# Result layout over the DMA parts, a gate half copied out by ScalarE, and a moved filter group in a GNN layer kernel

## The chip, the cores and the metric

The kernel runs on one core of a Trainium2 chip. The core has TensorE (PE in the profile; PEld is its weight load), VectorE (DVE), ScalarE (ACT), GpSimd (POOL) and SyncE (SP)[...]. Transfers are issued from SP and POOL here and run on 16 DMA engines. The metric is device time in microseconds for one execution of the whole program, less is better; the median of three runs before the change is 1708.58 us (1705.66 to 1714.0).

## The reference

`x` is 64 graphs of 256 nodes with 256 features, `adj` 64 matrices of 256 x 256. One layer is computed, all in float32:

```python
h = jnp.maximum(_layernorm(x, axis=-1), 0.0)
# convolution branch over the node axis
c = relu(bn(conv1d(h^T, conv1_w, 0)))
c = bn(conv1d(c, conv2_w, 8))                  # 17 taps
x_conv = relu(c + h^T)^T
# message branch
s = h @ w_se.T + b_se
A = exp(-dist(s, s)) * adj
x_nmp = A @ relu(h @ w_msg.T + b_msg)
# GRU cell, input is the two branches, state is h
gi = concat([x_conv, x_nmp]) @ w_ih.T + b_ih
gh = h @ w_hh.T + b_hh
r = sigmoid(gi_r + gh_r); z = sigmoid(gi_z + gh_z)
n = tanh(gi_n + r * gh_n)
return x + (1 - z) * n + z * h
```

## The kernel before

The 64 graphs are worked in 32 pairs, and four pairs make a batch (8 batches). Features lie on partitions in most of the work, so `HT[i]` holds pair i's `h` transposed, two chunks (`dc`) of 128 features by 512 columns.

The 17-tap convolution is done in a transformed domain. The taps are turned into filters once, at the start (`filters`, called by `filter_steps`), and written to DRAM (`filt`); each batch then reads them again, 47 loads of 256 KB into nine slots `wb` (`load_kinds`, `product`). In a batch `begin(m)` opens a product in a PSUM pair of banks `acc` (two of these, used in turn), ACT copies its first half to the second, and `complete(m)` adds two more products and lets ACT move the result out. The message branch (`message`, `embed`, `affinity`, `aggregate`) is spread between; it uses four single PSUM banks `aux` in turn and leaves `x_nmp` in `XNM[i]`, a ring of two tiles.

The gates of a pair are `gates(i)`: `seven` computes a 2 x 2 block product with seven block products, into `A` and `E` (the two `acc`), first for the gates r and z, then for the two halves of the gate n. `opened` is called when one of them is whole. For the gate n that is the inner function `n(dc, p)`, from line 1190: ACT takes one half of the PSUM tile with its bias into `gn`; VectorE multiplies it by r; VectorE adds the other half straight from PSUM; ACT applies tanh; three VectorE operations make the new state `d`, in `tr`; and two ACT copies of two-byte elements per `dc` split the words of `d` into their halves, in `back`. `finish(i)` then issues a DMA transpose on SP, `gn<-back`, and `deliver(i)` puts the halves together again (two ACT copies, `back<-gn`), adds `x` to it by two accumulating transfers on POOL, and writes the two graphs to `out` by two more. The last pair of a batch is delivered in the middle of the next batch; the last pair of all goes another way and isn't touched.

A row of `out` or `x` is brought onto partitions in one of two orders: `rows` (partition = 16 h + b) and `blocks` (partition = 8 b + h, which is the order of memory in pieces of two nodes). The access pattern of `rows` has 8 as its outermost dimension, that of `blocks` 16.

No instruction is issued where it is written. The class `Recorder` records every operation with an assumed cost, and `plan` orders them for all engines at once: TensorE in an order near the one written, the others by due times worked back from it, with a simple model of transfers in which `size` (line 346 for accumulating ones) is the time on the DMA engines. All instructions therefore have line 371 in the profile, and are told apart by their tiles.

At the start, pairs 0 to 3 are normalized, transposed and convolved one after the other, and `filter_steps` puts filter groups (line 1298) between them.

Of the kernel before, what the change touches and what calls it, by code (L numbers as in the profile page):

```python
# [14 lines left out]
U16 = mybir.dt.uint16  # L15
AF = mybir.ActivationFunctionType
ALU = mybir.AluOpType
# [232 lines left out]
class Recorder:  # L250
# [83 lines left out]
    def record(self, engine, op, args, kw):  # L334
        method = getattr(getattr(self.nc, engine), op)
        out = kw["out"] if "out" in kw else args[0]
        ins = [v for v in list(args) + list(kw.values()) if isinstance(v, bass.AP) and v is not out]
        n = 1
        for s in out.shape[1:]:
            n *= s  # L340
        size = 0
        if op.startswith("dma"):
            if "transpose" in op:
                size, cost = 2.5, self.TURN
            elif "accum_op" in kw:
                size, cost = 2.3, 1.0
            else:
                k = max(self.share(out, ins[0]), 10 if engine == "gpsimd" else 1)
                run = min(self.run(v) for v in (out, ins[0]))
                size = n * out.shape[0] * WIDTH[out.dtype] * 16 / k / 330e3 * max(1, 1400 / run)  # L350
                cost = 0.35 if k > 10 and run > 1024 else 0.62
        elif engine == "tensor":
            cost = n / 597 + 0.006
            if op == "transpose":
                cost = out.shape[-1] / 1170
            elif args[1].shape[0] < 32:
                cost = 0.23
        elif engine == "vector":
            cost = {"bn_stats": 0.33, "bn_aggr": 0.07}.get(op, n / 960 + 0.07)
            if op == "tensor_mul" and n == 256:  # L360
                cost = 0.5
        elif engine == "scalar":
            cost = n / 1400 + (0.2 if op == "activation" else 0.12)
            if out.dtype == U16:
                cost = n / 860
            elif len(out.shape) == 3 and op == "activation" and n == 256:
                cost = 0.49
        else:
            cost = 1.1 if self.planned == 0 else 7.0 if ALU.pow in args else 2.0
        k = len(self.tasks)  # L370
        self.tasks.append(Task(engine, lambda: method(*args, **kw), cost, size, self.first))  # L371
        self.last[engine] = k
        if self.behind is not None:
            self.tasks[k].preds.add(self.behind)
        if self.first is not None:
            self.first += 1
        for v in ins:
            self.access(k, v, False)
        self.access(k, out, True)
        return k  # L380
# [106 lines left out]
def kernel(  # L487
# [18 lines left out]
    nc = Recorder(tc.nc)  # L506
    P = 128
    B, N, D = x.shape
    G = 2
# [4 lines left out]
    DC = D // P  # L514
# [6 lines left out]
    L = 16  # L521
    NW = N // L
# [65 lines left out]
    def rows(t, g):  # L588
        return t[g].rearrange("(b h c) d -> h b (c d)", h=L // 2, c=MC)

    def row_tile(t, g):
        return t[:, g * MC:(g + 1) * MC, :].rearrange("p c d -> p (c d)")
# [5 lines left out]
    def chunk(t, g, c):  # L598
        return t[:, g * N + c * P:g * N + (c + 1) * P]
# [3 lines left out]
    X, ADJ, HT, XNM, STATS = {}, {}, {}, {}, {}  # L603
# [5 lines left out]
    def blocks(t, g):  # L609
        return t[g].rearrange("(b h c) d -> b h (c d)", h=L // 2, c=MC)  # L610
# [114 lines left out]
    p = aux()  # L725
# [449 lines left out]
    def halfs(p, k):  # L1175
        return p[:, :, k * N:(k + 1) * N]

    def pieces(t):
        return t.rearrange("p (g n) -> p g n", n=N)

    def gates(i, between=None):
        tr, gn = tr_tile, gn_tile
        tz = [slots[ROLE[f"tz{dc}"]].rearrange("p c d -> p (c d)") for dc in range(DC)]

        def rz(dc, p):
            for gate, t in ((0, tr[:, dc]), (1, tz[dc])):
                nc.scalar.activation(pieces(t), halfs(p, gate), AF.Tanh,
                                     bias=b_rz[:, gate * DC + dc:gate * DC + dc + 1], scale=0.5 - dc)

        def n(dc, p):  # L1190
            g = gn[:, dc]
            nc.scalar.activation(pieces(g), halfs(p, 1), AF.Identity,
                                 bias=b_hh[:, 2 * DC + dc:2 * DC + dc + 1], scale=1.0 - 2 * dc)
            nc.vector.scalar_tensor_tensor(g, tr[:, dc], 1.0, g, op0=ALU.add, op1=ALU.mult)
            nc.vector.scalar_tensor_tensor(pieces(g), pieces(g), 0.5, halfs(p, 0), op0=ALU.mult,
                                           op1=ALU.subtract if dc else ALU.add)
            nc.scalar.activation(g, g, AF.Tanh, bias=b_ih[:, 2 * DC + dc:2 * DC + dc + 1])
            d = tr[:, dc]
            nc.vector.tensor_sub(d, HT[i][:, dc], g)
            nc.vector.scalar_tensor_tensor(d, tz[dc], 1.0, d, op0=ALU.add, op1=ALU.mult)  # L1200
            nc.vector.scalar_tensor_tensor(d, d, 0.5, g, op0=ALU.mult, op1=ALU.add)
            u = d.bitcast(U16).rearrange("p (n j) -> p j n", j=2)
            for j in range(2):
                nc.scalar.copy(back.bitcast(U16).rearrange("p (c j n) -> p c j n", c=DC, j=2)[:, dc, j], u[:, j])

        def last(dc, g, p):
            a = slice(g * N, (g + 1) * N)
            v, d = gn[:, dc, a], tr[:, dc, a]
            nc.scalar.activation(v, p[:, N:], AF.Identity,
                                 bias=b_hh[:, 2 * DC + dc:2 * DC + dc + 1], scale=1.0 - 2 * dc)  # L1210
            nc.vector.scalar_tensor_tensor(v, d, 1.0, v, op0=ALU.add, op1=ALU.mult)
            nc.vector.scalar_tensor_tensor(v, v, 0.5, p[:, :N], op0=ALU.mult, op1=ALU.subtract if dc else ALU.add)
            nc.scalar.activation(v, v, AF.Tanh, bias=b_ih[:, 2 * DC + dc:2 * DC + dc + 1])
            nc.vector.tensor_sub(d, HT[i][:, dc, a], v)
            nc.vector.scalar_tensor_tensor(d, tz[dc][:, a], 1.0, d, op0=ALU.add, op1=ALU.mult)
            for c in range(MC):
                t = chunk(y_last[:, dc], g, c).rearrange("p (b h) -> p h b", b=NW)
                u, w = (q[:, c * P:(c + 1) * P].rearrange("p (h b) -> p h b", b=NW) for q in (d, v))
                nc.vector.scalar_tensor_tensor(t, u, 0.5, w, op0=ALU.mult, op1=ALU.add)

        seven(i, RZ, rz)
        if between:
            between()
        if i + 1 < NP:
            seven(i, NH, n)
            return
        a0, p5, e1, a1, e0 = aux(), aux(), aux(), acc()[:, 1], acc()[:, 0]
        e = slots[ROLE["e"]].rearrange("p c d -> p (c d)")
        part(a0, 1, i, NH, True)
        nc.scalar.mul(e0, a0, -1.0)  # L1230
        part(p5, 5, i, NH, True)
        nc.scalar.copy(e, p5)
        part(a0, 2, i, NH)
        last(0, 0, a0)
        part(e0, 6, i, NH)
        nc.vector.tensor_add(a1, e0, e)
        part(e0, 7, i, NH)
        nc.vector.scalar_tensor_tensor(e1, e0, -1.0, e, op0=ALU.mult, op1=ALU.subtract)
        last(1, 1, e1)
        part(a1, 3, i, NH)  # L1240
        last(0, 1, a1)
        part(e0, 4, i, NH)
        last(1, 0, e0)
# [16 lines left out]
    def deliver(i):  # L1260
        y = back.rearrange("p (q d) -> p q d", d=D)
        t = gn_tile.rearrange("p c n -> p (c n)").bitcast(U16)
        v = y.bitcast(U16).rearrange("p q (c d j) -> p j c q d", c=DC, j=2)
        u = t.rearrange("p (c j q d) -> p j c q d", j=2, c=DC, d=P)
        for j in range(2):
            nc.scalar.copy(v[:, j], u[:, j])
        for g in range(G):
            nc.gpsimd.dma_start(out=row_tile(y, g), in_=rows(x, G * i + g), accum_op=ALU.add)
            nc.gpsimd.dma_start(out=rows(out, G * i + g), in_=row_tile(y, g))

    FIRST = PARTS[1][1]
    steps = deque((m, g) for g in range(FIRST) for m in range(len(PASSES)))
# [5 lines left out]
    def filter_steps(n, wide=True):  # L1278
        for _ in range(n):
            banks[0] += 1  # L1280
            p = acc()[:, 0] if wide and banks[0] % 3 == 0 else aux()
            filters(p, *steps.popleft(), nc.gpsimd if len(steps) % 2 else nc.sync)
# [9 lines left out]
    for j in range(PB):  # L1292
        if j > 0:
            norm(j)
        transpose_h(j)
        conv1(j, True)
        split(j)
        filter_steps((1, 2, 3, 3)[j])
    *bn2, b_ih, b_hh = columns("bn2")
    s2, h2_shift = fold_bn(bn2, "bn2", 1.0 / L)  # L1300
    b_rz = keep("b_rz", 2 * DC)
# [19 lines left out]
    for b in range(NB):  # L1321
        i = b * PB
# [25 lines left out]
        if b == 0:  # L1348
# [6 lines left out]
            back = late.tile([P, DC * W], FP, name="back")  # L1355
# [168 lines left out]
```

## Time and profile before

| | |
|---|---|
| runs | 1705.66, 1714.0, 1708.58 us |
| profiled execution | 1703.87 us |
| its span, first to last instruction | 1702.1 us |
| mean granted TensorE clock | 0.994 |
| POOL and SP transfers: `back<-in_x_dram`, `out_dram<-back` | 62 each, 256 KB |
| filter loads `wb<-filt` | 376, 256 KB |

A view of the instructions in order of time gives start, length, engine, tile written and read, and in brackets the idle time of that engine before, with what ended it. Where an instruction waits for several semaphores, the bracket names only one.

### The profile page before, as it was taken

How to read it: one execution, taken by the hardware profiler on the slowest of the kernel's cores; microseconds unless marked ns; L12 is line 12 of the kernel's file. 1: busy time of each engine (PE TensorE's matmuls, PEld its weight loads, DVE VectorE, ACT ScalarE, POOL GpSimd, SP SyncE). 2: the span in 40 equal slices, each digit the busy share in tenths (PEclk: the TensorE clock that was granted, in tenths of full speed). 3: DMA queues.
4: the chain of work that ended last, by engine and by line, in shares of the span. 5: the costliest groups of instructions: out<-in, count | busy, mean ns of one | idle time of the engine just before them, and what ended most of it. 6: DMA issues, size and time to landing. Idle time of an engine off the chain costs nothing.

```text
span 1702.1 us, 26181 instructions
## 1 busy us (share of the span) xinstructions
PE 1666.3 (98%) x8984; PEld 1420.8 (83%) x8984; DVE 1457.8 (86%) x3401; ACT 1052.4 (62%) x1967; POOL 231.8 (14%) x245
## 2 busy tenths in 40 slices
PE   8999999999999999999999999999999999999998
PEld 5888878988889788888888887897888978898886
DVE  7969989799889998799997998979987899879545
ACT  5546665685657765676655866567575766556453
POOL 4211130022110121102110021101211012100010
PEclk9999999999999999999999999999999999999999
DMA  9982666966579366773559554694756836484032
GB/s 228 306 280 69 137 117 142 280 136 140 108 196 241 94 127 124 218 208 89 122 113 293 136 116 110 160 273 97 144 112 191 233 91 125 88 245 129 17 60 52
DMA packets 326812, 261.47 MB, mean 154 GB/s; under 512 B 204751, under 2 KB 252139, under 8 KB 326678
## 3 DMA queue, kind: packets, MB, share of 16 engines
q1 hardware_dynamic: 296982, 216.71, 48.4%
q0 software_dynamic: 29280, 42.76, 13.1%
q8 instruction: 71, 1.16, 0.3%
q14 instruction: 63, 0.52, 0.1%
q10 hardware_dynamic: 416, 0.32, 0.1%
HBM read 156.60 MB, written 43.78 MB: 118 GB/s over the span
## 4 chain that ended last, share of the span: by engine, by line
PE 77%; DVE 17%; DMA 3%; issue 1%; ACT 1%; SPq 0%; DVEq 0%; ACTq 0%
PE acc L371 52%; PE aux L371 25%; DVE V L371 3%; DVE T L371 3%; DVE U L371 2%; DVE gn L371 2%; DMA wb<-filt 2%; DVE tr L371 1%; DVE acc L371 1%; DVE wb L371 1%; DVE Yv L371 1%; DVE PT L371 1%; DMA taps<-in_c_wT_dram 1%; DVE msg L371 1%; DMA filt<-Yv 0%
## 5 line engine op out<-in xcount | busy, mean ns | idle before, releaser
L371 PE MATMUL acc<-wb,w_ih 128*128 128x256 f32 x768 | 191.9, 379 | 0.0
L371 PEld LDWEIGHTS acc<-wb,w_ih 128*128 128x128 f32 x768 | 145.9, 190 | 19.8
L371 POOL DMA_DIRECT2D back<-in_x_dram x62 | 61.9, 1161 | 696.6 <-ACT back L371 622.5
L371 POOL TENSOR_TENSOR rstd<-rstd,neg_half 128x4 f32<-128x4 f32 x32 | 81.6, 2548 | 472.7 <-DVE shift L371 284.8
L371 PE MATMUL aux<-wb,w_x 128*128 128x256 f32 x576 | 141.6, 384 | 0.6 <-ACT e L371 0.5
L371 DVE SCALAR_TENSOR_TENSOR V<-T,V 128x128 f32<-128x128 f32 (+2 forms) x448 | 140.2, 377 | 0.0
L371 PE MATMUL acc<-wb,w_x 128*128 128x256 f32 x576 | 136.5, 381 | 1.8 <-DVE acc L371 1.5
L371 PEld LDWEIGHTS acc<-wb,w_x 128*128 128x128 f32 x576 | 107.9, 190 | 28.6 <-DVE acc L371 8.4
L371 PEld LDWEIGHTS aux<-wb,w_x 128*128 128x128 f32 x576 | 108.0, 191 | 20.2 <-issue 4.0
L371 PE MATMUL aux<-w_msg,hT 128*128 128x259 f32 x512 | 120.9, 381 | 0.0
L371 PE MATMUL acc<-V,wb 128*128 128x128 f32 x1024 | 119.0, 275 | 0.6 <-ACT acc L371 0.6
L371 PEld LDWEIGHTS acc<-U,wb 128*128 128x128 f32 x1024 | 117.4, 192 | 1.5 <-issue 0.5
L371 PE MATMUL acc<-U,wb 128*128 128x128 f32 x1024 | 118.2, 275 | 0.3 <-DMA wb<-filt 0.3
L371 PEld LDWEIGHTS acc<-V,wb 128*128 128x128 f32 x1024 | 116.7, 192 | 1.2 <-ACT acc L371 0.8
L371 PE MATMUL acc<-wb,w_hh 128*128 128x256 f32 x384 | 110.1, 381 | 0.7 <-ACT acc L371 0.7
L371 DVE TENSOR_TENSOR T<-Yv 128x512 f32<-128x512 f32 (+1 forms) x80 | 42.5, 580 | 79.4 <-ACT Yv L371 78.9
L371 PE MATMUL aux<-hT,w_c 128*128 128x512 f32 x224 | 107.3, 595 | 2.7 <-ACT e L371 2.7
L371 PE MATMUL acc<-Yv,w_ih 128*128 128x256 f32 x380 | 108.5, 381 | 0.1
L371 PEld LDWEIGHTS aux<-w_msg,hT 128*128 128x128 f32 x512 | 96.5, 190 | 14.3
L371 PE MATMUL acc<-hT,w_hh 128*128 128x256 f32 x380 | 104.7, 383 | 0.6 <-ACT acc L371 0.4
L371 PE MATMUL acc<-xnm,w_ih 128*128 128x256 f32 x380 | 103.9, 380 | 0.0
L371 ACT COPY back<-gn 128x1024 uint16<-128x1024 uint16 x62 | 80.5, 1348 | 36.6 <-DMA gn<-back 36.6
(194 smaller groups left out, 3842.1 us busy)
## 6 DMA issues: line engine op xcount, KB each, us to landing
wb<-filt SPq DMA_DIRECT2D x376, 256.0 KB
back<-in_x_dram POOLq DMA_DIRECT2D x62, 256.0 KB, 7.3
out_dram<-back POOLq DMA_DIRECT2D x62, 256.0 KB, 4.8
x<-in_x_dram SPq DMA_DIRECT2D x58, 256.0 KB
halves_d<-halves SPq DMA_DIRECT2D x28, 512.0 KB
adjh<-halves_d SPq DMA_DIRECT2D x112, 128.0 KB
hh<-halves SPq DMA_DIRECT2D x108, 128.0 KB
filt<-Yv POOLq DMA_DIRECT2D x18, 224.0 KB, 4.6
```

The costliest lines, as they stand in the source:

```text
L371: self.tasks.append(Task(engine, lambda: method(*args, **kw), cost, size, self.first))
```

## The change

Four edits. The results go to memory and are added to `x` in `blocks` order, for which the last two copies in `n` reorder the columns while they write. In `n`, ACT copies the second half of the gate out of PSUM into `XNM[i][:, dc]` (which is no longer needed there), and VectorE reads that instead of PSUM. The first filter group at the start is asked for after the second pair, not after the first, and one group more after the fourth. The planner's assumed `size` of an accumulating transfer goes from 2.3 to 1.3.

```diff
             elif "accum_op" in kw:
-                size, cost = 2.3, 1.0
+                size, cost = 1.3, 1.0
...
             nc.scalar.activation(pieces(g), halfs(p, 1), AF.Identity,
                                  bias=b_hh[:, 2 * DC + dc:2 * DC + dc + 1], scale=1.0 - 2 * dc)
+            x = XNM[i][:, dc]
+            nc.scalar.copy(pieces(x), halfs(p, 0))
             nc.vector.scalar_tensor_tensor(g, tr[:, dc], 1.0, g, op0=ALU.add, op1=ALU.mult)
-            nc.vector.scalar_tensor_tensor(pieces(g), pieces(g), 0.5, halfs(p, 0), op0=ALU.mult,
-                                           op1=ALU.subtract if dc else ALU.add)
+            nc.vector.scalar_tensor_tensor(g, g, 0.5, x, op0=ALU.mult, op1=ALU.subtract if dc else ALU.add)
...
             u = d.bitcast(U16).rearrange("p (n j) -> p j n", j=2)
+            v = back.bitcast(U16).rearrange("p (c j n) -> p c j n", c=DC, j=2)[:, dc]
             for j in range(2):
-                nc.scalar.copy(back.bitcast(U16).rearrange("p (c j n) -> p c j n", c=DC, j=2)[:, dc, j], u[:, j])
+                nc.scalar.copy(v[:, j].rearrange("p (q b h) -> p q h b", h=L // 2, b=NW),
+                               u[:, j].rearrange("p (q h b) -> p q h b", h=L // 2, b=NW))
...
         for g in range(G):
-            nc.gpsimd.dma_start(out=row_tile(y, g), in_=rows(x, G * i + g), accum_op=ALU.add)
-            nc.gpsimd.dma_start(out=rows(out, G * i + g), in_=row_tile(y, g))
+            nc.gpsimd.dma_start(out=row_tile(y, g), in_=blocks(x, G * i + g), accum_op=ALU.add)
+            nc.gpsimd.dma_start(out=blocks(out, G * i + g), in_=row_tile(y, g))
...
-        filter_steps((1, 2, 3, 3)[j])
+        filter_steps((0, 2, 3, 4)[j])
```

## The prediction

> **What bounds the kernel now.** I read the page first, then who made TensorE (PE) wait, then the instructions in order of time around the longest waits on PE, SP, POOL and ACT.
>
> ```profile
> span 1702.1 us, 26181 instructions
> PE 1666.3 (98%) x8984; PEld 1420.8 (83%) x8984; DVE 1457.8 (86%) x3401; ACT 1052.4 (62%) x1967; POOL 231.8 (14%) x245
> ```
>
> PE is the bound: 1702.1 - 1666.3 = 35.8 us is all that any rearrangement can win. The view of who waited for whom, for PE alone, shows where most of it lies:
>
> ```profile
> PE acc L371 <- DVE tr L371: 9.4, 4, 2.4
> PE acc L371 <- DMA wb<-filt: 3.1, 4, 1.9
> PE aux L371 <- DMA taps<-in_c_wT_dram: 2.7, 1, 2.7
> PE acc L371 <- DVE gn L371: 1.8, 1, 1.8
> ```
>
> The reader should see that four waits of 2.3 to 2.4 us are put down to VectorE. In the instructions in order of time they all stand at one place, the start of a batch (`begin(0)`, first filter product); PE, SP and POOL at the fourth such place:
>
> ```profile
> 896.78 1.04 PE L371 MATMUL aux<-w_msg,hT 128*128 128x259 f32 x4
> 900.22 3.81 PE L371 MATMUL acc<-Sv,wb 128*128 128x128 f32 x32 [2.40 <-DVE tr L371]
> ...
> 893.52 20.01 SPq L371 DMA_DIRECT2D wb<-filt  x23
> ...
> 886.80 1.96 POOL L371 DMA_DIRECT2D back<-in_x_dram  x2 [27.11 <-ACT back L371]
> 893.27 0.64 POOL L371 DMA_DIRECT2D out_dram<-back  x1 [4.51 <-DMA back<-in_x_dram]
> 895.89 0.63 POOL L371 DMA_DIRECT2D out_dram<-back  x1 [1.99 <-DMA back<-in_x_dram]
> ```
>
> The named releaser is misleading. The matmul waits for several semaphores, and the one that is last but for the start itself is the landing of a filter load. Of the sixteen completion marks of the load issued at 893.96, eight come at 896.61 to 897.38 and eight at 898.61 to 900.09; PE starts at 900.22. The result write issued at 893.27 has the same split: eight marks at 896.0 to 896.7, eight at 898.0 to 899.5. So the write sits on half of the DMA engines, and a filter load that needs all sixteen waits for that half. The six places and their waits are 296.45 (1.75), 497.11 (2.28), 697.76 (1.95), 900.22 (2.40), 1101.01 (2.36), 1301.79 (2.36): 13.1 us. The seventh, near 1500, shows under 1 us.
>
> [...] `rows` has an outer dimension of 8, `blocks` of 16 or, merged, 128. The marks above agree with 8. [...] the copy into `zT` stored at a stride of 32 bytes (first four pairs) against the same shape stored densely (later pairs).
>
> ```profile
> L371 ACT COPY zT<-aux x2: 312/355/398, 81.9 to 82.1; 128x128 f32<-128x128 f32 x1, 32x128 f32<-32x128 f32 x1
> ...
> L371 ACT COPY zT<-aux x1: 283/283/283, 304.9 to 304.9; 128x128 f32<-128x128 f32 x1
> ...
> L371 ACT COPY back<-tr x124: 596/618/632, 194.0 to 1671.4; 128x512 uint16<-128x512 uint16 x124
> ```
>
> The first row's 398 ns is the 128x128 form; the four strided ones are 383 to 407 ns, the dense ones of the same places in the batch 254 to 283.
>
> **Part 1, results in block order.** It moves no bytes away; each `back<-in_x` and `out_dram<-back` (62 each, 256 KB) puts 16 KB on sixteen engines instead of 32 KB on eight.
>
> ```profile
> back<-in_x_dram POOLq DMA_DIRECT2D x62, 256.0 KB, 7.3
> out_dram<-back POOLq DMA_DIRECT2D x62, 256.0 KB, 4.8
> ```
>
> At the batch start: the two adds are issued at 886.80 and 887.42 and land at 892.98 and 895.15. Unused engines gave their marks after 2.2 us, so about 4 us of the first add is transfer; halved, it lands near 891 and the second near 893. In the new instruction order ACT runs both `back<-gn` copies ahead of the four `tr`/`tz` evictions (before, two evictions stood between them: 2 x 0.6 us), which brings the adds another 1 us or more forward. The writes then go out near 890 and 892 and half as long per engine, so they are mostly through when the load issued at 893.96 is served; its undelayed half landed by 897.4, before PE is free at 897.82. I take a rest of 0.25 us at each place: 6 x 0.25 = 1.5, a gain of 13.1 - 1.5 = 11.6 us. Bounds: nothing (the half-loaded sixteen collide as badly, a gain of perhaps a third, 4 us) to 13.1. VectorE is not next: the first `acc` is read out by 897.8 and the second half of the gate now is copied out by ACT (part 2).
>
> The price is in the `back<-tr` copies. They now store two-byte elements 16 bytes apart, 124 of them. With a fixed part of 188 ns (the copies of 12 elements into `z` take that), `back<-tr` runs at 0.86 ns an element, `back<-gn` with stores 4 bytes apart at (1348-188)/1024 = 1.13, and the strided `zT` at about 1.74. For 512 elements 1.13 gives 0.77 us, 1.74 gives 1.08. I take 1.02, a growth g of 0.40 us each[...]; bounds 0.15 and 0.46, up to 0.7 if the many short rows cost too (`h<-aux`, rows of 16, takes 782 ns where dense 512-element evictions take about 600). ACT gains 124 x 0.40 = 50 us of work. Most lies in idle time: ACT is at 62%. Two places are tight. Once in each of six batches (440 to 1447), four copies stand right before the exponentials that free the `aux` buffers:
>
> ```profile
> 1039.96 2.17 ACT L371 COPY back<-tr 128x512 uint16<-128x512 uint16 x4
> 1043.28 1.21 ACT L371 ACTIVATE e<-aux 128x256 f32<-128x256 f32 x4 [1.15 <-PE aux L371]
> ...
> 1043.72 1.12 PE L371 MATMUL aux<-hT,w_c 128*128 128x512 f32 x2 [0.45 <-ACT e L371]
> ```
>
> The slack is 1.15 us, of which part 2's copies eat about 0.35; beyond 0.8 each delay of `e` goes to PE directly: 4g - 0.8 = 0.8 us. After a batch start, the four copies stand around the two `Yv<-acc` evictions (before: 904.61 to 906.78), and the second eviction frees the `acc` that `begin(3)` wants at 913.76. Its slack of 1.26 us shrinks because PE runs 2.3 us earlier while the copies still wait for VectorE; I get about 2.2g - 0.2 = 0.7 us. Together 6 x (6.2g - 1.0) = 37g - 6: 8.9 us at g = 0.40, nothing below g = 0.16, 11 at 0.46, 20 at 0.7. The other two groups of four in a batch have 2 to 6 us of idle ACT behind them and cost nothing; without that cover each would cost up to 1.6 us.
>
> **Part 2, gate copied out by ACT.** Adds 62 copies of 128x512 from PSUM; `acc<-acc` of that form takes 575 ns: 35.7 us of ACT. VectorE's product then reads SBUF; `tr<-wb,tr`, all SBUF, takes 679 ns, the PSUM one 677, so nothing. It removes no wait of length: outside the batch starts PE's waits for VectorE at `acc` sum to under 2 us. Behind the copies in ACT's queue stand the evictions of the next pair, which have idle time of 0.5 to 2.7 us ahead of them. Cost beyond the 0.35 us above: 0; bounds -1 to +2 us.
>
> **Part 3, filter group and planner cost.** The first group's wait is for the second `taps` load, landing at 18.69 (PE 18.82, 2.68 us idle). In the new order the transposes come before and the whole group still stands ahead of the second pair's convolution, so PE waits for the same landing with the same work done: 0, bounds -0.5 to +0.5. On SP the `gn<-back` transpose (913.70, 3.32 us) leaves the middle of the filter loads for a place after them; it hid under loads running ahead: 0, bounds -1 to +1. The first batch start has its own new order on SP (an `adj` transpose ahead of the filter loads, in a gap of 12 us before 290.40): 0, bounds -1 to +2.
>
> **Sum.** -11.6 + 8.9 = -2.7 us. Against the profiled execution, 1703.87 (span 1702.1), that is 1701.2. The median of the three runs is 1708.58, 4.7 higher, so there 1705.9.
>
> **Rivals.** Faster: strided stores are cheap (g at or below 0.2). For it: two-byte elements are not four-byte ones, and the `zT` copies are short. Then 37 x 0.2 - 6 = 1.4 and the time is 11.6 - 1.4 = 10.2 lower, 1698. Slower: ACT's queue becomes what PE waits for; one mechanism, the strided copies ahead of `e` and of `Yv<-acc`. At g = 0.75 it costs 21.8, so +10 us, 1719; it outweighs the gain from g = 0.48 and passes +8.5 us from g = 0.71, or from g = 0.5 if the loads still land late (gain 4 only). For it: the rows of 16. Against: 62% ACT. The change does not do what it says: the DMA stays on eight engines or the loads are late for their own length; then only the cost stays, -4 + 8.9 = +5, within the bound. Part 3 is such a case already.
>
> **How the numbers follow.** What one measurement can tell here is about 0.5%, 8.5 us. Forecast (within it) 0.52, with the case of loads still late in it; cheap stores 0.28; ACT bound 0.20. The likeliest case alone: 1700 to 1715. Range 1695 to 1718: it takes in most of the faster case and the lower half of the slower one.
>
> **What would show it.** Right: the waits of about 2.3 us before `acc<-Sv,wb` at six batch starts fall under 0.6; `back<-tr` near 1.0 us; the wait before `aux<-hT,w_c` grows from 0.45 to about 1.2; the `taps` wait stays 2.6. Wrong: `back<-tr` at 0.7 or 1.3; batch starts still at 2 us; new waits of PE for ACT elsewhere.

## The result, and the profile after

The changed kernel takes 1891.94 us (median of 4 runs, 1884.66 to 1896.84) beside 1707.12 us for the kernel before (4 runs, 1702.95 to 1714.0): a ratio of 1.1075, 95% interval 1.1019 to 1.1131. It is 10.8% slower, where 1706 was forecast with a range up to 1718.

The group of the `back<-tr` copies in the kernel before (busy time in us, mean ns of one, idle time before):

```profile
L371 ACT COPY back<-tr 128x512 uint16<-128x512 uint16 x124 | 68.9, 617 | 18.4 <-DVE tr L371 18.4
```

The head of the page of the changed kernel and its busy times, then its costliest group and two rows of the DMA part:

```profile
span 1895.1 us, 26235 instructions
...
PE 1729.3 (91%) x8984; PEld 1465.3 (77%) x8984; DVE 1461.6 (77%) x3401; ACT 1295.1 (68%) x2029; POOL 241.0 (13%) x245
...
L371 ACT COPY back<-tr 128x512 uint16<-128x512 uint16 x124 | 295.4, 2651 | 16.9 <-DVE tr L371 16.7
...
back<-in_x_dram POOLq DMA_DIRECT2D x62, 256.0 KB, 5.3
out_dram<-back POOLq DMA_DIRECT2D x62, 256.0 KB, 2.6
```

PE was 98% busy and is 91% now. One `back<-tr` copy takes 2.65 us where it took 0.62, and the copies fill 295.4 us of ACT where they filled 68.9. (295.4 is less than 124 x 2.651 because one copy begins before the last has quite ended, as at 781.52, where one of 2.46 us is followed by the next at 783.49; a copy holds ACT's queue for 295.4 / 124 = 2.38 us, before for 0.56.) The two transfers land in 5.3 and 2.6 us where they took 7.3 and 4.8, so the sixteen parts do what was meant. ACT is still only 68% busy: its share of busy time does not show that it has become the limit. The view of who made PE wait does (us in total, times, longest):

```profile
PE acc L371 <- ACT wb L371: 39.1, 11, 5.5
PE aux L371 <- ACT e L371: 36.4, 10, 7.0
PE acc L371 <- ACT Yv L371: 35.6, 11, 5.2
PE acc L371 <- ACT acc L371: 22.0, 9, 3.5
PE acc L371 <- DVE acc L371: 14.6, 11, 5.0
...
PE aux L371 <- DMA taps<-in_c_wT_dram: 2.9, 1, 2.9
```

The four rows for ACT hold 133 us; before, the largest row of all was 9.4. The wait for `taps` is still there, as predicted. Of the waits for a filter load at the batch starts, 13.1 us before, none over 0.25 us is left ahead of a batch's first filter product; PE waits for filter loads in two other places, 1.7 us in all (0.44 at 116.27, and 1.28 at 1229.93 ahead of a batch's second filter product). In the transfers' marks at the batch start near 1216, the writes issued at 1215.29 and 1217.27 have landed at 1217.76 and 1219.63, the sixteen marks of each within 0.24 us of one another, and all sixteen marks of the filter loads issued at 1220.55 and 1220.98 come within 0.4 us of one another.

ACT and PE in order of time, at the place that the prediction showed at 1039.96 in the kernel before:

```profile
1149.80 9.28 ACT L371 COPY back<-tr 128x512 uint16<-128x512 uint16 x4
...
1158.59 1.52 ACT L371 ACTIVATE e<-aux 128x256 f32<-128x256 f32 x4
...
1159.35 1.22 PE L371 MATMUL aux<-hT,w_c 128*128 128x512 f32 x1 [6.78 <-ACT e L371]
```

The four copies take 9.28 us instead of 2.17, the exponentials behind them come that much later, and PE, which needs the `aux` bank that they empty, stands for 6.78 us instead of 0.45. From this wait back to the same wait one batch earlier (930.62) lie four other waits, 4.88, 0.94, 5.15 and 2.65 us, and a small one of 0.45. With the 6.78 that is 20.9 us in a batch, beside 2.9 in the kernel before (2.40 and 0.45, from 842.88 to 1043.72). A batch is 228.7 us long instead of 200.8: 27.9 more, and the waits explain 18.0 of it. PE's busy time, 207.9 us in this batch and 198.0 in that one, explains the other 9.9, for the same work.

That rest is TensorE's clock, 0.94 in the mean of this batch and 1.00 in that one. Busy time of each engine in stretches of 7 us that begin where a wait ends, for the changed kernel (columns: stretch; its length; PE, PEld, DVE, ACT and POOL busy with their instructions; granted PE clock; DMA share; GB/s). The waits ahead of the five stretches were 2.65, 6.78, 4.87, 4.96 and 0.45 us:

```profile
1110.70:1117.70 7.00, 7.00 (x26) 5.94 (x27) 3.17 (x6) 6.20 (x4) 4.22 (x2) 0.79 0.19 36
1159.40:1166.40 7.00, 7.00 (x18) 5.08 (x19) 4.14 (x12) 5.63 (x7) 0.00 (x0) 0.61 0.54 116
1210.70:1217.70 7.00, 7.00 (x20) 5.71 (x21) 2.39 (x10) 1.60 (x3) 2.80 (x4) 0.61 0.61 112
...
1245.00:1252.00 7.00, 7.00 (x40) 7.00 (x41) 6.97 (x14) 4.69 (x10) 0.00 (x0) 0.63 0.33 89
1078.80:1085.80 7.00, 7.00 (x32) 6.19 (x33) 7.00 (x19) 4.41 (x7) 2.72 (x1) 1.00 0.11 38
```

After the waits of 4.87, 4.96 and 6.78 us PE is counted as busy, but at 0.61 to 0.63 of its clock over the next 7 us; after 2.65 us at 0.79; after 0.45 at 1.00. From 1118 to 1124 and from 1166 to 1168, behind two of these stretches, it was 1.00 again. By an estimate from these rows, each long wait thus costs 7 x 0.38 = 2.7 us beyond its own length, and a batch loses 7 x (0.39 + 0.39 + 0.37 + 0.21) = 9.5 us so, which is nearly all of the 9.9. How the length of a wait sets the clock behind it is not shown. Over the whole run the mean granted clock fell from 0.994 to 0.951, and PE's busy time grew from 1666.3 to 1729.3 us with the same 8984 matmuls.

### The profile page after: what moved, and what is told of

The parts are those of the page before. It is cut to its first block, busy times and chain, and to the rows that moved or that the text cites. A ratio compares the mean times of both kernels' runs of the same rounds, so it can differ in the third digit from the quotient of the medians.

```text
span 1895.1 us, 26235 instructions
## 1 busy us (share of the span) xinstructions
PE 1729.3 (91%) x8984; PEld 1465.3 (77%) x8984; DVE 1461.6 (77%) x3401; ACT 1295.1 (68%) x2029; POOL 241.0 (13%) x245
## 4 chain that ended last, share of the span: by engine, by line
PE 55%; ACT 20%; DVE 15%; DMA 5%; issue 5%; SPq 0%; ACTq 0%; DVEq 0%
PE acc L371 37%; PE aux L371 18%; ACT back L371 13%; DVE tr L371 3%; DVE wb L371 3%; DMA gn<-back 2%; DVE gn L371 2%; DVE V L371 2%; ACT hT L371 1%; ACT zT L371 1%; DVE T L371 1%; ACT gn L371 1%; ACT wb L371 1%; DVE acc L371 1%; DVE Yv L371 1%
## 5 line engine op out<-in xcount | busy, mean ns | idle before, releaser
L371 ACT COPY back<-tr 128x512 uint16<-128x512 uint16 x124 | 295.4, 2651 | 16.9 <-DVE tr L371 16.7
L371 PE MATMUL acc<-wb,w_ih 128*128 128x256 f32 x768 | 196.6, 386 | 0.0
L371 POOL DMA_DIRECT2D back<-in_x_dram x62 | 56.5, 1054 | 918.5 <-ACT back L371 881.4
L371 PE MATMUL acc<-hT,w_hh 128*128 128x256 f32 x380 | 114.6, 412 | 56.1 <-ACT wb L371 39.1
L371 POOL TENSOR_TENSOR rstd<-rstd,neg_half 128x4 f32<-128x4 f32 x32 | 98.9, 3090 | 479.3 <-DVE shift L371 249.1
L371 PE MATMUL acc<-wb,w_x 128*128 128x256 f32 x576 | 146.0, 402 | 3.8 <-DVE acc L371 3.6
L371 PEld LDWEIGHTS acc<-wb,w_x 128*128 128x128 f32 x576 | 115.9, 203 | 36.6 <-DVE acc L371 9.1
L371 PEld LDWEIGHTS acc<-hT,w_hh 128*128 128x128 f32 x380 | 73.8, 204 | 85.5 <-ACT wb L371 43.5
L371 PE MATMUL aux<-w_msg,hT 128*128 128x259 f32 x512 | 126.8, 395 | 0.0
L371 DVE TENSOR_TENSOR acc<-acc,wb 128x512 f32<-128x512 f32 x64 | 44.9, 701 | 95.9 <-PE acc L371 87.6
```

## Experiments

### Which part, and what of it

The dense-store version is the changed kernel with the two copies walked in the order of the destination, so that stores are dense and reads jump:

```diff
-                nc.scalar.copy(v[:, j].rearrange("p (q b h) -> p q h b", h=L // 2, b=NW),
-                               u[:, j].rearrange("p (q h b) -> p q h b", h=L // 2, b=NW))
+                nc.scalar.copy(v[:, j].rearrange("p (q b h) -> p q b h", h=L // 2, b=NW),
+                               u[:, j].rearrange("p (q h b) -> p q b h", h=L // 2, b=NW))
```

> The changed kernel with one thing undone: the four back<-tr copies of a pair visit the elements in the order of the destination (q, b, h), so they write densely and read at a stride instead. Same result, same order of instructions on every engine. Theory A (the 2.65 us of a copy come from its stores, and the time is lost because ACT's queue holds back what PE waits for): back<-tr about 0.6 to 0.8 us, no wait of PE for ACT over 1 us, granted clock back at 0.99, and about 11 us under the kernel before, 1695. Theory B (the gate's copies out of PSUM and the new order on ACT are the cost): still over 1800. Theory C (the turned pattern is slow whichever side is strided): back<-tr over 2 us, 1890.

Part 1 alone is the kernel before with `rows` made `blocks` in the two DMAs and the turning copies as changed, nothing else:

```diff
-                nc.scalar.copy(back.bitcast(U16).rearrange("p (c j n) -> p c j n", c=DC, j=2)[:, dc, j], u[:, j])
+                nc.scalar.copy(v[:, j].rearrange("p (q b h) -> p q h b", h=L // 2, b=NW),
+                               u[:, j].rearrange("p (q h b) -> p q h b", h=L // 2, b=NW))
...
-            nc.gpsimd.dma_start(out=row_tile(y, g), in_=rows(x, G * i + g), accum_op=ALU.add)
-            nc.gpsimd.dma_start(out=rows(out, G * i + g), in_=row_tile(y, g))
+            nc.gpsimd.dma_start(out=row_tile(y, g), in_=blocks(x, G * i + g), accum_op=ALU.add)
+            nc.gpsimd.dma_start(out=blocks(out, G * i + g), in_=row_tile(y, g))
```

> The kernel before with the first part alone: results in block order, copies with strided stores; nothing else. Theory A: all of the loss is here, 1870 to 1900, back<-tr 2.65 us. Theory B: within 20 us of the kernel before.

The version in rows is the changed kernel with these lines put back (part 1 undone; parts 2 and 3 and the planner's number stay).

> The changed kernel without its first part: results in the old row order over 8 DMA parts and the old dense copies; the gate's copies, the moved filter group and the planner's number stay. Theory A: within 5 us of the kernel before, batch starts still waiting about 2 us each, so 1700 to 1710, and the difference to the run with dense writes is what the sixteen parts are worth: 10 to 13 us. Theory B: over 1800.

Part 1 alone: 1887.18 us, ratio 1.1077 (1.105 to 1.1105), the whole loss, as theory A had it. Without part 1: 1706.96, ratio 1.0004 (0.9993 to 1.0015), so parts 2 and 3 together are nothing, as predicted. The waits of 1.2 to 2.6 us at its batch starts are there again. Dense stores: 1708.32, ratio 1.0009 (0.9996 to 1.0021); its group and PE's waits:

```profile
L371 ACT COPY back<-tr 128x512 uint16<-128x512 uint16 x124 | 126.3, 1073 | 14.8 <-DVE tr L371 14.6
```

```profile
PE aux L371 <- ACT e L371: 9.9, 10, 1.5
...
PE acc L371 <- ACT Yv L371: 3.3, 5, 0.8
PE acc L371 <- DMA wb<-filt: 3.2, 7, 0.6
```

The order in which the same 512 elements are stored makes 2.65 us of 1.07 and decides the whole 184 us. The waits for filter loads are short here too. But the time is not below before, and theory A, right about the stores, missed with 1695: it had put a copy at 0.6 to 0.8 us and no wait for ACT over 1 us. The copies still cost more than plain ones, and what the loads gave shows again as waits for `e` (up to 1.5 us) and `Yv`. Whether that is the full account, the kernels further down tell.

### Is it ACT's queue, or something that the strided stores do to others?

The changed kernel with plain dense copies, each issued four times over (the columns stay unturned):

```diff
+                k = nc.scalar.copy(v[:, j], u[:, j])
+                nc.repeat(k, 4)
```

> The changed kernel with each back<-tr copy in its old dense form but issued four times in a row, so that ACT's queue is held for about as long (4 x 0.54 = 2.2 us instead of 2.65) with no strided store. The columns are not reordered, so the nodes of the output come out permuted. Theory A (queue time alone): 1830 to 1890, PE's waits for ACT at the same places, granted clock 0.95 to 0.97. Theory D (strided stores also slow PE's own reads of SBUF, which is where the 63 us more of PE busy time come from): PE busy near 1666, granted clock 0.99, and time under 1800.

It takes 1908.77 us (two runs), ratio 1.1187 (1.1158 to 1.1215), with

```profile
L371 ACT COPY back<-tr 128x512 uint16<-128x512 uint16 x496 | 299.8, 617 | 29.0 <-DVE tr L371 16.9
```

as much time in ACT's queue as in the changed kernel (299.8 beside 295.4 us), and no strided store. The same waits appear (`e` 40.4 us, `wb` 40.8, `Yv` 40.4), PE's busy time is 1730.0 and its clock 0.950. That rules theory D out; the time is somewhat above the range of theory A. So the time in ACT's queue is enough to make the loss; that the stores disturb VectorE or a transfer is not needed to explain it, and VectorE's busy time does not show it (1457.8 before, 1461.6 after).

### Why a copy takes 2.65 us

The kernel before with 48 copies added behind its end, twelve forms four times each, told apart by their element counts; they write only tiles that are no longer used.

> The kernel before with 48 ScalarE copies added after its last instruction, four of each of twelve forms, told apart by their element counts; two-byte and four-byte elements, dense and with stores 4, 8, 16 and 32 bytes apart, and the turned pattern of the change. Their own durations are what is looked at. Theory A [...]: 16-byte and 32-byte stride of two-byte elements about 5 ns an element without any turned pattern, 4 bytes about 1.1; four-byte elements at 16 and 32 bytes about 1.7. Theory C (the turned pattern and its short rows): the plain strides stay under 2 ns an element for both sizes, and the turned form is slow for four-byte elements too; the turned read with dense stores (448 elements) is then slow as well.

The groups of these copies by form (busy time of the four, and mean ns of one). Two-byte forms: 512 stored densely from every second element; 504, 500, 248 and 120 stored at a stride of 4, 8, 16 and 32 bytes; 480 stored in the turned pattern of the change; 448 stored densely from a turned source. Four-byte forms: 496 dense; 492, 252 and 124 at a stride of 8, 16 and 32 bytes; 416 stored in the turned pattern, which for them is a stride of 32 bytes.

```profile
L371 ACT COPY back<-tr 128x480 uint16<-128x480 uint16 x4 | 9.3, 2322 | 0.1
L371 ACT COPY back<-tr 128x500 uint16<-128x500 uint16 x4 | 5.2, 1296 | 0.1
L371 ACT COPY back<-tr 128x248 uint16<-128x248 uint16 x4 | 5.1, 1286 | 0.1
L371 ACT COPY back<-tr 128x448 uint16<-128x448 uint16 x4 | 3.8, 942 | 0.1
L371 ACT COPY back<-tr 128x416 f32<-128x416 f32 x4 | 3.7, 935 | 0.1
L371 ACT COPY back<-tr 128x504 uint16<-128x504 uint16 x4 | 3.0, 751 | 0.1
L371 ACT COPY back<-tr 128x120 uint16<-128x120 uint16 x4 | 2.8, 692 | 0.1
L371 ACT COPY back<-tr 128x252 f32<-128x252 f32 x4 | 2.5, 634 | 0.1
L371 ACT COPY back<-tr 128x492 f32<-128x492 f32 x4 | 2.5, 628 | 0.1
L371 ACT COPY back<-tr 128x512 uint16<-128x512 uint16 x4 | 2.5, 620 | 0.6 <-DVE tr L371 0.5
L371 ACT COPY back<-tr 128x496 f32<-128x496 f32 x4 | 2.4, 604 | 0.1
L371 ACT COPY back<-tr 128x124 f32<-128x124 f32 x4 | 1.6, 412 | 0.1
```

With 0.188 us taken off as a fixed part, as in the prediction (an estimate from the copies of 12 elements, 188 ns), and the rest divided by the elements, a two-byte element costs 0.84 ns dense, 1.1 at a stride of 4 bytes, 2.2 at 8, 4.4 at 16 and 4.2 at 32. A four-byte element costs 0.84 dense, 0.89 at 8, 1.8 at 16 and 1.8 at 32. The turned pattern costs what the plain stride costs, with both widths (480 two-byte elements 4.4 ns, 416 four-byte ones 1.8), so its short rows add nothing: theory A, not theory C. For two-byte elements, then, the price doubles from 4 to 8 and again from 8 to 16 bytes of stride, and ends 2.5 times as high as that of four-byte elements. Reads that jump are far cheaper: 448 elements from 56 bytes apart took 1.7 ns each. The turned copy of 512 at 4.4 ns would be 0.19 + 2.25 = 2.44 us; in the kernel the copies took 2.46 to 2.84 us, 2.65 in the mean, and where the last 0.2 comes from was not tried. Nor is it shown why ACT's two-byte stores are dearer.

### What the landing is worth, and how the price grows

Three more give the price at other sizes. First the changed kernel with plain copies and the sixteen parts kept (the strided copy replaced by `nc.scalar.copy(v[:, j], u[:, j])`): the landing without its price.

> The changed kernel with the back<-tr copies plain again (two-byte elements stored densely, in the order they come) and the sixteen-part DMAs kept, so the nodes of the output stand in another order: the turning is left out. This is part 1's DMA with none of its price. Theory A (the landing gain is real, and the dense-store version loses it again on ACT, 1.07 us a copy against 0.62): back<-tr at 0.62 us, PE's waits for ACT e and ACT Yv of the dense-store version (9.9 and 3.3 us) fall to those of the row version (about 5 and under 1), the batch-start waits stay under 0.6 us; time about 11 us under before, 1694 to 1697. Rival B (the waits at the batch starts were only in the place of others): the waits move elsewhere or the PE idle total stays near 30 us, and the time is within 3 us of before, 1703 to 1709.

Then the version of repeated copies with `nc.repeat(k, 2)`:

> As the version whose copies are dense and issued four times over, but twice only: each copy takes 2 x 0.62 us of ACT, a growth of 0.65 us with the gap between them (the node order of the output is left turned). Theory A (the loss is queue time on ACT in two tight places a batch, as the prediction's formula 37g - 6 had it, until the slack of the other places is gone near g = 1): 37 x 0.65 - 6 = 18 us of cost, less 11 for the landing, 1713 to 1717. Rival C (all the places are tight from the start; straight line from the dense-store version at g = 0.46 to the changed kernel at g = 2.03): about 1708 + 0.2 x 117 = 1731, clock visibly under 0.99.

And the dense-store version with part 2 undone:

```diff
-            x = XNM[i][:, dc]
-            nc.scalar.copy(pieces(x), halfs(p, 0))
...
-            nc.vector.scalar_tensor_tensor(g, g, 0.5, x, op0=ALU.mult, op1=ALU.subtract if dc else ALU.add)
+            nc.vector.scalar_tensor_tensor(pieces(g), pieces(g), 0.5, halfs(p, 0), op0=ALU.mult,
+                                           op1=ALU.subtract if dc else ALU.add)
```

> The dense-store version without part 2 (VectorE reads the gate's second half out of PSUM again), so ACT has 62 x 0.6 = 36 us less to do. Theory A (the copies of part 2 eat into the slack ahead of e, 0.35 us or more at each of the batches): PE's wait for ACT e falls from 1.5 to about 0.9 us a batch, the time to about 1702 to 1705. Rival B (part 2 costs nothing, the e wait is all from the dearer back<-tr copies): 1707 to 1709, the e wait unchanged.

With free sixteen parts: 1691.3 us, ratio 0.9913 (0.9896 to 0.9931), about 15 us under before. Theory A holds and the gain is larger than the 11.6 us of the sum. Two rows of PE's waits there:

```profile
PE aux L371 <- ACT e L371: 4.5, 10, 0.5
...
PE acc L371 <- DMA wb<-filt: 2.6, 6, 0.7
```

Between the profiled executions (1702.1 and 1689.7) the span falls by 12.4: PE's busy time by 5.6, from 1666.3 to 1660.7, and its idle time by 6.8. So less idle time went than the 11.6 us of the sum. At the first batch start a wait of 1.59 us for ACT's `zT` stands where 1.75 us for a load stood, and several small waits grew (those for `e` from 3.2 to 4.5 us in total). The other part of the gain is the clock: in the kernel before, two of the six batch-start waits (697.76 and 1301.79) were followed by a clock of 0.76 over 7 us, 2 x 7 x 0.24 = 3.4 us by an estimate.

With the copies twice over: 1728.85 us, ratio 1.0135 (1.0106 to 1.0165). Rival C, the straight line, was nearer (1731) than the formula (1713 to 1717). The waits by themselves were close to the prediction's: the one for `e` is 2.34 us in a batch, 1.9 more than in the version with free sixteen parts (4g - 0.8 = 1.8 at g = 0.65), and the one for `Yv` 1.1 to 1.6 in three batches (2.2g - 0.2 = 1.2). PE's idle time (span less busy time) was 19.7 us above that version's, near what the formula has (18). But PE's busy time rose as well, by 11.0 from 1660.7 to 1671.7, and the time by 30.7 us between the two profiled spans, 37.6 in the medians.

The rows of the price, all in ACT's queue time for one copy (busy time of the group divided by 124) above the plain 0.56, and relative to the version with free sixteen parts by the ratios at 1707 us: dense stores 0.46 us, cost 16 us; twice over 0.63, cost 38; the changed kernel 1.83, cost 198; four times over 1.86, cost 217. The formula 37g - 6 gives 11, 17, 62 and 63. It is low by about a third at the dense stores, near the size it was made for, and by three times at the size that the copies turned out to have.

Without part 2 the dense-store version takes 1704.57, ratio 0.9993 (0.998 to 1.0007), beside 1.0009 (0.9996 to 1.0021) with it. The wait for `e` falls from 9.9 to 7.0 us in total. That fits theory A's direction; the two intervals overlap, so a cost of part 2 is not shown.

### A way to the gain without the price

One of the two copies of a gate on POOL, the other on ACT, both with dense stores; and the same without part 2:

```diff
+                if j:
+                    nc.gpsimd.tensor_copy(a, b)
+                else:
+                    nc.scalar.copy(a, b)
```

> The dense-store version (stores dense, reads turned), with one of the two copies of each gate (j = 1) on POOL and the other on ACT: the whole computation is done. No row shows what POOL takes for such a copy. Theory A (what is lost is ACT's queue time only): ACT has 1.07 us a gate where the plain copies have 2 x 0.62, so PE's waits for ACT e and Yv are those of the version with plain copies (4.5 us and under 1 us), and the time lies within 5 us of its 1691, 1690 to 1697, as long as POOL's copy stays under about 2 us. Rival B (POOL's copy is slow, or holds VectorE up, and the transposed result comes late): POOL over 2.5 us a copy or VectorE's rows longer, new waits for POOL back, 1702 or more.

> As the run with half of the copies on POOL, and part 2 undone (VectorE reads the gate's second half out of PSUM). Theory A (part 2 costs some slack ahead of e and brings nothing): 1 to 3 us less than the run with part 2. Rival B (part 2 is nothing once ACT has room): the two agree within 2 us.

1731.13 us, ratio 1.0134 (1.0117 to 1.0151), and 1733.39, ratio 1.0144 (1.0122 to 1.0166): rival B of the first as to the time, and no difference made by part 2. From the view of one tile, the copies on POOL (min, median and max in ns), and from PE's waits:

```profile
L371 POOL COPY back<-tr x62: 1035/1395/7009, 194.3 to 1698.8; 128x512 uint16<-128x512 uint16 x62
```

```profile
PE acc L371 <- ACT wb L371: 14.2, 7, 2.1
PE acc L371 <- DVE acc L371: 11.2, 17, 2.0
PE aux L371 <- ACT e L371: 5.4, 12, 0.5
```

The wait for `e` is short again, but a copy on POOL takes between 1.0 and 7.0 us, and the transposed result comes late. POOL and ACT ahead of one of the waits for `wb`:

```profile
1094.48 8.15 POOL L371 COPY back<-tr 128x512 uint16<-128x512 uint16 x2 [12.99 <-DVE tr L371]
...
1107.01 1.35 ACT L371 COPY back<-gn 128x1024 uint16<-128x1024 uint16 x1 [7.66 <-DMA gn<-back]
```

The transpose is issued at 1102.65, behind POOL's two copies; ACT, which has `back<-gn` next in its queue, stands for 7.66 us; and PE waits 2.00 us at 1111.22 for an eviction that ACT does after it. VectorE's busy time is 1487.1 us where the dense-store version has 1459.6. `U<-T,U` lengthened (368 ns in the mean, 325 in the kernel before), `V<-T,V` did not (375 and 377). What spreads POOL's copies from 1.0 to 7.0 us, and whether VectorE's 27 us come from them, is not shown.

Then the kernel before, without any of the four edits, and its DMAs cut by columns, in the expectation that the two halves of a transfer lie on different engines.

```diff
+            for c in range(MC):
+                a, b = slice(c * D, (c + 1) * D), row_tile(y, g)
+                nc.gpsimd.dma_start(out=rows(out, G * i + g)[:, :, a], in_=b[:, a])
```

In the first kernel the adds are cut in the same way as the writes, in the second the writes alone.

> The kernel before with each add and each write cut into its two column halves (1 KB a row each), one DMA behind the other on POOL: no turning of columns, plain copies, 124 more DMA issues on each of the two sorts. The whole computation is done. Theory A (each half sits on eight DMA engines, the next half on the next eight, so that no engine has more than 16 KB of one result ahead of a filter load): batch-start waits for wb<-filt under 1 us as in the version with free sixteen parts; time 1692 to 1700. Rival B (both halves sit on the same eight engines, or packets of 1 KB and twice the issues cost as much): the waits of 2 us at the batch starts stay, 1703 to 1712.

> The kernel before with the writes alone cut into column halves, the adds whole. Theory A (the late marks of the filter loads come from the write alone): as much gained as with both cut, 1692 to 1700. Rival B (the add's transfer on eight engines is what brings the write late into the filter loads): half of it or nothing, 1700 to 1709.

Both cut: 1708.07, ratio 1.0016 (1.0006 to 1.0027). Its batch-start waits for loads are gone, but six waits of 1.49 us for ACT's `z` (8.9 us in total) stand in their place: in the order that the planner now made, a transposition of `z` comes ahead of the filter products there. So theory A of this run is right about the loads and wrong about the time. The writes alone: 1696.32, ratio 0.9943 (0.9921 to 0.9966), 8 to 10 us under before and in the range of theory A, with nothing added to ACT. Its span, busy times, plain copies and PE's largest wait:

```profile
span 1689.7 us, 26291 instructions
...
PE 1661.2 (98%) x8984; PEld 1417.9 (84%) x8984; DVE 1458.7 (86%) x3401; ACT 1049.2 (62%) x1967; POOL 254.6 (15%) x307
```

```profile
L371 ACT COPY back<-tr x124: 598/618/641, 193.5 to 1658.8; 128x512 uint16<-128x512 uint16 x124
```

```profile
PE acc L371 <- DMA wb<-filt: 4.2, 9, 1.0
```

This version beats both kernels by some 0.6% and 10%. Around 890 the marks of its filter loads come within about 1.3 us of one another, the two groups of eight are gone, and of the batch starts one still waits over 1 us (1.72 at 496.88). The planner also placed the adds of that batch earlier (881.37 instead of 886.80), so how much is due to the halves and how much to the new order was not separated. Nor is it shown which engines took the halves.

## Why the prediction was wrong, by its steps

**What bounds the kernel, and the landing: right in the mechanism, in part lucky in the size.** PE waited for filter loads at six places. At five of them the marks of the load come in two groups of eight, 1.2 to 1.4 us apart (897.38 and 898.61 at the place that the prediction showed); at the first, 296.45, they do not part so clearly. That results in block order would use all sixteen engines was the author's estimate; the sixteen marks within 0.24 us of both writes near 1216 in the changed kernel agree with it. How an engine shares its time between a write and a load was not shown. The sixteen parts took these waits away. The gain was put at 11.6 us, all of it idle time. Without its price it measured 15 (12.4 between the profiled spans): only 6.8 us of idle time, and 5.6 us of PE's busy time, which the prediction had taken as fixed when it called 35.8 us all that any rearrangement can win.

**The price of the copies: the step that failed.** "I take 1.02, a growth g of 0.40 us each" and "bounds 0.15 and 0.46, up to 0.7". Measured: 2.65, a growth of 2.03. The figure came from two-byte stores 4 bytes apart (`back<-gn`) and from four-byte stores 32 bytes apart (`zT`), taking it that a store at a given stride costs the same whatever the width of the element; of the 0.77 and 1.08 us that follow from the two, to go up to 1.02 was the author's estimate. (Its 1.74 ns for `zT` is a little high too: (398 - 188) / 128 is 1.64, and 0.86 for the plain copy should be 0.84. Neither matters here.) Two-byte stores 16 bytes apart cost 4.4 ns an element, four-byte ones 1.8. The four-byte rows are flat up to 8 bytes (0.84 and 0.89 ns) and double at 16; the two-byte rows rise already at 4 and 8 bytes (1.1 and 2.2). The dense-store version had nearly the size that was assumed (1.07 us) and took 1708.32 us, 2 us from the forecast, but by two errors that cancel: its gain was 15 us instead of 11.6 and its cost 16 instead of 11. With the right duration of this one instruction the same sum gives 37 x 2.03 - 6 - 11.6 = 57 us slower: the right side, but a third of what was measured.

**The cover: the step that failed next.** "The other two groups of four in a batch have 2 to 6 us of idle ACT behind them and cost nothing." At 0.46 us of growth that holds nearly; at 2.03 a group of four grows by some 7 us (2.17 to 9.28), more than the idle time behind it, and the waits of 2.65 and 4.87 us in each batch belong to these two groups. The price was a straight line made at one point, with two places in it; the caveat, "without that cover up to 1.6 us each", was for that same small growth.

**The clock: missing.** The sum took a wait at its own length. In the changed kernel each of the three long ones in a batch costs 2.6 to 2.7 us more by the estimate from the stretches of 7 us, a third of the loss (9.5 of 27.9 us in a batch).

**The slower rival** was the right mechanism (ACT's queue) and half of the places: the waits for `e` and `Yv` hold 72 of the 133 us, those for `wb` and `acc` the rest. It had 0.20 of the chance, and its 1719 us was far too low. **Part 2, part 3 and the moved transposes** were put at nothing, and the run without part 1 shows them so. The signs named beforehand answered: batch starts under 0.6 and `taps` at 2.9 as on the right side, 6.78 instead of 1.2 ahead of `aux<-hT,w_c`, and two under "wrong", a copy above 1.3 and new waits for ACT elsewhere.

## What to carry to other kernels

An access pattern is part of an instruction's price, here 0.62, 1.07 or 2.65 us for the same 512 elements: before a permutation is put on a copy, look for a row with the same element width and the same stride on the same side, and if there is none, let the upper bound be a multiple. If one side has to jump, let it be the read (here 1.7 ns an element for a jumping read, 4.4 for a jumping store). ACT, 62% busy, had slack only between particular instructions, 1.15 us of it ahead of `e`, so a price formula holds for the growth at which the slack was counted. The waits of PE of 2.65 to 6.78 us seen here cost 1.5 to 2.7 us more than their length, by the same estimate. And before a layout is turned on a compute engine for the sake of a DMA, try to cut the DMA: here the writes in two halves along the row came with 8 to 10 of the 15 us and asked nothing of ACT, though a new order came with them.

## What had not been expected of the hardware

ACT's two-byte stores at a stride of 16 bytes cost 4.4 ns an element against 0.84 dense, and 2.2 already at 8 bytes, where four-byte stores still cost 0.89. Waits of PE of 4.87 to 6.78 us left it at 0.61 to 0.63 of its clock over the next 7 us; shorter waits went either way. After the six batch-start waits of 1.75 to 2.40 us in the kernel before it was 1.00 four times and 0.76 twice, over 7 us; after five waits of 2.32 to 2.34 us in the run with copies twice over, 1.00 twice (at 851.01, for one) and 0.76 to 0.78 three times (at 1054.58, for one). The same copy on POOL took anything from 1.0 to 7.0 us.
